# Attention scores by head, the mask carried as extra contraction rows, and row maxima from the high parts only

## The chip, the cores and the metric

The kernel runs on one core of a Trainium2 chip. The metric is the device time of one execution in microseconds (us). Work is spread over five engines that run side by side: TensorE (PE, matmuls; its weight loads are listed as PEld), VectorE (DVE), ScalarE (ACT), GpSimd (POOL) and SyncE (SP), which issues most of the DMA copies.

## The reference

One pre-norm transformer block in float32 over x of shape 4 x 2048 x 256:

```
x = x + attention(layernorm(x), Wq, Wk, Wv, Wo)
x = x + ffn(layernorm(x), W1, b1, W2, b2)
```

Attention has 16 heads of 16 dimensions. A query sees its own position and the 63 before it: `allowed = (j <= i) & (j > i - 64)`; scores are divided by 4 and go through a softmax. The FFN has 1024 hidden units with relu; its weights are rounded to -1, 0 or 1 by `clip(round(W / (mean|W| + 1e-5)))` in the kernel.

## The kernel before

Tokens are cut into 32 chunks of 256 (`C`), eight to a sequence; a chunk has four blocks of 64 queries (`W`, `NB = 4`). Every float32 factor is split into a float16 high part and a float16 low part (`hl`, `ph` and `pl`, `hh` and `hl`, `ht`, `op2`), and a product is the sum of two or three float16 matmuls.

The stages of a chunk, by function:

- `load` and `norm_in`: x comes in as `xt`; `layernorm` (statistics on DVE, a power on POOL at L505, normalisation on DVE at L521 or ACT at L517, high part on ACT at L523, low part on POOL or DVE at L537); a transposing DMA (L545) makes `xT`.
- `project`: q, k and v, twelve matmuls of 256 columns each (L575, L567). High parts are taken on ACT (L619, L585), low parts on DVE (L621, L589). q is written with its block index innermost, so with a step of four float16. q and k go to DRAM (`qd`, `kd`), three copies of 256 rows each, by two DMAs each (L626, L629). v is kept as `vo`, and `ve` is v shifted by one block, made by DMAs (L593, L595, L601).
- `stack`: four DMAs (L650, L656) read q and k back, with the heads in pairs. In `qst` and `kst` a pair has 96 rows: 48 for one head (three high and low combinations of 16 rows) and 48 for the other, with zeros where a head's rows meet the other head's queries. So one matmul gives exact scores of two heads. There are three such buffers (`NQ = 3`), and `stack(c)` waits until the weights of chunk c-3 are done (`used`).
- `maxima`: per block eight matmuls (L675), 128 rows of two heads' queries by 128 keys. The window of 64 keys that a query sees is a ring: a predicated copy (L680) puts the old keys in the place of the new keys that a query may not see, and a reduction (L693) takes the maxima. After four blocks the negated maxima are transposed (L704), copied (L707) and go through DRAM (`md`, issued by ACT at L709 and by POOL at L712) into row 96 of `qst`, where row 96 of `kst` is constant: the next scores come out with their maximum already subtracted.
- `weights`: per block and half of the heads, one matmul writes the mask into the bank (L729, the identity times 512 columns) and four more add transposed scores, keys by queries (L732, 97 rows, 128 columns each):

```
nc.tensor.matmul(tpf, identb, msk.rearrange("p a q -> p (a q)"), start=True, stop=False)
for i in range(4):
    p = g * 4 + i
    nc.tensor.matmul(tp[:, i], ks[0:97, p, b * W:b * W + 128], qs[0:97, p, :, :, b], start=False, stop=i == 3)
```

  ACT takes the exponential and the high part `ph` (L742 and L745, or L751 and L753); the low part `pl` is a subtraction on POOL (L747) or DVE (L755). `lanes.pick` chooses when the program is built.
- `values`: 24 matmuls (L780 to L782) with `ph` and `pl` as stationary operands and v as the moving one; ACT copies out (L787), DVE inverts the sums (L793), POOL multiplies (L805).
- `wo_out`: two transposing DMAs (L828), twelve matmuls (L839), the residual (L843), the second layernorm, a transposing DMA (L855).
- `ffn1` and `ffn2`: the first layer for two chunks at a time (L888 for the bias b1, L892), relu on ACT (L905), low part on DVE (L907); the second layer per chunk (L929, L930) after a one-row product that puts b2 into the bank (L927), the residual (L935) and the store (L938).

The order of the work is not that of the loops. Each stage is a generator that yields what it needs next (an engine with a cost, a buffer, an event); `Lanes.run` plays them against a model of the engines when the program is built, takes the step that can start first, and by `PRIO` among equals. `Lanes.chain` then fixes this order on every engine, SP included. `BUFS` holds the numbers of buffers.

Of the kernel before, what the change touches and what calls it, by code (L numbers as in the profile page):

```python
# [20 lines left out]
D = 256  # L21
# [14 lines left out]
NQ = 3  # L36
NFIRST = 0
NLAST = 6
PRIO = {'norm': -1.1, 'proj': 0.4, 'max': 0.2, 'att': 2.9, 'val': -2.2, 'wo': 0.6, 'ffn': 5.5, 'ffn2': 5.6, 'prep': 3.6}
BUFS = {'xt': 9, 'ln': 2, 'xT': 3, 'zT': 2, 'qk': 4, 'vp': 4, 'pp': 8, 'op': 2, 'av': 2, 'o': 1, 'h': 10, 'r': 7, 'bank': 4, 'lin': 6, 'sp': 2, 'tp': 3, 'pv': 4}  # L40
# [6 lines left out]
WT = {'P': 1.126, 'A': 1.0, 'D': 0.902, 'G': 0.95, 'S': 0.0}  # L47
# [151 lines left out]
def kernel(ctx: ExitStack, tc: tile.TileContext, x, Wq, Wk, Wv, Wo, W1, b1, W2, b2, out):  # L199
# [18 lines left out]
    qkp = pool("qkp", BUFS["qk"])  # L218
# [31 lines left out]
    qd = dram.tile([3, D, NCH * C], HP, name="qd")  # L250
    kd = dram.tile([3, D, NCH * C], HP, name="kd")
    md = dram.tile([NCH, NP, 4 * 2 * W], HP, name="md")
# [3 lines left out]
    identb = const.tile([128, 128], BF, name="identb")  # L256
    mhalf = const.tile([128, NT], FP, name="mhalf")
    zb = const.tile([128, W], FP, name="zb")
    zh = const.tile([48, C], HP, name="zh")
    ones = const.tile([128, 128], FP, name="ones")  # L260
    onesh = const.tile([128, W], HP, name="onesh")


    qst = [const.tile([128, NP, 2, W, 4], HP, name=f"qst{i}") for i in range(NQ)]
    kst = [const.tile([128, NP, W + C], HP, name=f"kst{i}") for i in range(NQ)]
    mst = [const.tile([NP, 128, 4], HP, name=f"mst{i}") for i in range(NQ)]

    b1r = const.tile([33, FF], HP, name="b1r")
    b2r = const.tile([33, D], HP, name="b2r")
# [5 lines left out]
    tri = const.tile([128, W], U8, name="tri")  # L275
    sel = const.tile([128, W], HP, name="sel")
    neg = const.tile([128, W], FP, name="neg")
    mask = const.tile([128, 8, W], BF, name="mask")
    mask0 = const.tile([128, 8, W], BF, name="mask0")

    xts, xTs, vs, ps_, hs, wts = {}, {}, {}, {}, {}, {}
# [3 lines left out]
    def constants():  # L285
        yield "G", 0.4
        make_identity(nc, ident)
        yield "D", 0.6
        nc.vector.memset(mhalf, -0.5)
        nc.vector.memset(zb, 0.0)  # L290
        nc.vector.memset(zh, 0.0)
        nc.vector.memset(ones, 1.0)
        nc.vector.memset(onesh, 1.0)
        signal("const")
        yield "D", 0.3
        nc.vector.tensor_copy(identh, ident)
        nc.vector.tensor_copy(identb, ident)
        signal("ident")

    def masks():  # L300
        yield wait("ident")
        yield "G", 0.8

        for h in range(2):
            r = slice(h * 64, h * 64 + 64)
            nc.gpsimd.affine_select(sel[r], onesh[r], [[1, W]], ALU.is_gt, 0.0, base=0, channel_multiplier=-1)

        mf = const.tile([128, W], FP, name="mf")
        nc.gpsimd.affine_select(mf[0:64], zb[0:64], [[-1, W]], ALU.is_gt, -BIG, base=0, channel_multiplier=1)
        nc.gpsimd.affine_select(mf[64:128], zb[64:128], [[1, W]], ALU.is_ge, -BIG, base=0, channel_multiplier=-1)  # L310
        yield "D", 0.6
        nc.vector.tensor_copy(tri, sel)
        nc.vector.memset(neg, -BIG)
        yield "D", 1.2
        nc.vector.tensor_copy(mask, mf.unsqueeze(1).to_broadcast([128, 8, W]))
        nc.vector.memset(mask0[0:64], -BIG)
        nc.vector.tensor_copy(mask0[64:128], mf[64:128].unsqueeze(1).to_broadcast([64, 8, W]))
        signal("masks")

    def stacks(i):  # L320
        yield wait("const")
        for h in range(2):
            yield "S", (0.65, 1.1)
            nc.sync.dma_start(
                out=qst[i][48 * h:48 * h + 48, :, 1 - h].rearrange("r p q b -> r p (q b)"),
                in_=zh.unsqueeze(1).to_broadcast([48, NP, C]),
            )
        for a in range(0, NP, 2):
            yield "G", 0.57
            nc.gpsimd.memset(kst[i][96:97, a:a + 2], SW * SW)  # L330
        yield "G", 0.5
        nc.gpsimd.memset(mst[i], 0.0)
        signal("used", i - NQ)

# [8 lines left out]
    def weight_qkv(nm):  # L343
# [12 lines left out]
        whv, wlv = wh, wl  # L356
        if nm != "v":
            whv = wh.rearrange("p d (r j) -> p d j r", r=HD)
            wlv = wl.rearrange("p d (r j) -> p d j r", r=HD)
        for d in range(2):  # L360
            wpv = wp[:, d] if nm == "v" else wp[:, d].rearrange("p (j r) -> p j r", r=HD)
            yield "A", 0.3
            nc.scalar.activation(whv[:, d], wpv, AF.Copy, scale=SW)
            yield "D", 0.34
            nc.vector.scalar_tensor_tensor(wlv[:, d], wpv, SW, whv[:, d], ALU.mult, ALU.subtract)
# [4 lines left out]
    def weight_o():  # L370
# [19 lines left out]
        yield "D", 0.6  # L390
# [4 lines left out]
    def biases():  # L395
        yield "G", 0.6
        nc.gpsimd.memset(oner, 1.0)
        nc.gpsimd.memset(b1r, 0.0)
        nc.gpsimd.memset(b2r, 0.0)
        for b, br, n in ((b1, b1r, FF), (b2, b2r, D)):  # L400
# [91 lines left out]
    def layernorm(src):  # L492

        yield wait("const")
        yield "D", 1.07
# [8 lines left out]
        yield "G", 0.63  # L504
# [3 lines left out]
        onact = lanes.pick([[("D", 0.65)], [("D", 0.07), ("A", 1.0)]])  # L508
        xn = rp.tile([128, 2, NT, 128], FP, name="r")
        ht = lnp.tile([128, 2, 2, NT, 128], HP, name="ht")  # L510
        if onact:
            yield "D", 0.07
            nb = small.tile([128, NT], FP, name="nb")
            nc.vector.scalar_tensor_tensor(nb, mv[:, :, 0], -1.0, rs, ALU.mult, ALU.mult)
            for t in range(NT):
                yield "A", 0.5
                nc.scalar.activation(xn[:, :, t, :], src[:, t, :].rearrange("p (d n) -> p d n", d=2), AF.Identity, scale=rs[:, t:t + 1], bias=nb[:, t:t + 1])  # L517
        else:
            yield "D", 0.65
            for t in range(NT):  # L520
                nc.vector.tensor_scalar(xn[:, :, t, :], src[:, t, :].rearrange("p (d n) -> p d n", d=2), mv[:, t, 0:1], rs[:, t:t + 1], ALU.subtract, ALU.mult)  # L521
        yield "A", 0.52
        nc.scalar.copy(ht[:, 0], xn)  # L523
        yield from low([(ht[:, 1], xn, ht[:, 0])], 0.6, 1.11)
# [27 lines left out]
    def project(c, nm):  # L552
# [26 lines left out]
        if nm == "v":  # L579
# [4 lines left out]
            yield "A", 0.48  # L584
# [3 lines left out]
            yield "D", 0.6  # L588
# [21 lines left out]
        yield get("qk")  # L610
        hl = qkp.tile([128, 2, 2, C], HP, name="hl")
        hiv, lov, psv = hl[:, 0], hl[:, 1], ps
        if nm == "q":

            hiv = hl[:, 0].rearrange("p e (q b) -> p e b q", b=4)
            lov = hl[:, 1].rearrange("p e (q b) -> p e b q", b=4)
            psv = ps.rearrange("p e (b q) -> p e b q", b=4)
        yield "A", 0.48
        nc.scalar.copy(hiv, psv)  # L619
        yield "D", 0.6  # L620
        nc.vector.tensor_tensor(lov, psv, hiv, ALU.subtract)  # L621
        put("lin")

        two = 0 if nm == "q" else 1
        yield "S", (0.48, 0.36, 2.05)
        nc.sync.dma_start(out=dst[2 - 2 * two, :, t0:t0 + C].rearrange("(e p) t -> p e t", p=128), in_=hl[:, 0])  # L626
        lanes.cur[0] = lanes.free["S"]
        yield "S", (0.48, 0.73, 2.05)
        nc.sync.dma_start(  # L629
            out=dst[two:two + 2, :, t0:t0 + C].rearrange("s (e p) t -> p (s e) t", p=128),  # L630
            in_=hl.rearrange("p s e t -> p (s e) t"),
        )
        put("qk")
        signal(nm, c)

    def stack(c):
        first = c % NCB == 0
        yield wait("q", c)
        yield wait("k", c)
# [3 lines left out]
        if first:  # L643
            yield "G", 0.46
            nc.gpsimd.memset(ks[0:96, :, 0:W], 0.0)
        lo0 = 0 if first else W
        for ab in range(2):
            rows = slice(48 * ab, 48 * ab + 48)
            yield "S", (0.65, 0.55)
            nc.sync.dma_start(  # L650
                out=qs[rows, :, ab].rearrange("r p q b -> r p (q b)"),
                in_=qd[:, :, t0:t0 + C].rearrange("s (r p a) t -> a (s r) p t", a=2, r=HD)[ab],
            )
            lanes.cur[0] = lanes.free["S"]
            yield "S", (0.65, 0.68)
            nc.sync.dma_start(  # L656
                out=ks[rows, :, W - lo0:],
                in_=kd[:, :, t0 - lo0:t0 + C].rearrange("s (r p a) t -> a (s r) p t", a=2, r=HD)[ab],
            )
            if ab == 0:  # L660
                lanes.cur[0] = lanes.free["S"]
        signal("stack", c)
        for b in range(NB):
            start("max", c, maxima(c, b), 2 * b)
            start("val", c, values(c, b), b)

    def scores(c, b):

        qs, ks = qst[c % NQ], kst[c % NQ]
        yield wait("masks")  # L670
        yield get("sp")
        yield "P", 0.44
        sp = sps.tile([128, NP, 128], FP, name="sp")
        for p in range(NP):
            nc.tensor.matmul(sp[:, p, :], qs[0:96, p, :, :, b], ks[0:96, p, b * W:b * W + 128], start=True, stop=True)  # L675
        yield "D", 0.6
        old = sp[:, :, 0:W]
        if c % NCB == 0 and b == 0:
            old = neg.unsqueeze(1).to_broadcast([128, NP, W])
        nc.vector.copy_predicated(sp[:, :, W:128], tri.unsqueeze(1).to_broadcast([128, NP, W]), old)  # L680
        return sp[:, :, W:128]
# [5 lines left out]
    def maxima(c, b):  # L687
        ring = yield from scores(c, b)
        yield "D", 0.68
        if ("mx", c) not in ps_:  # L690
            ps_["mx", c] = small.tile([128, NB, NP], FP, name="mx")
        mx = ps_["mx", c]
        nc.vector.tensor_reduce(mx[:, b], ring, AX.X, ALU.max)  # L693
        put("sp")
        if not tally(("max", c), NB):
            return
        yield "D", 0.2
        mh = small.tile([128, NB, NP], HP, name="mh")
        nc.vector.tensor_scalar(mh, mx, -1.0 / (SW * SW), PSHIFT * 4.0, ALU.mult, ALU.add)
# [282 lines left out]
```

## Time and profile before

| | |
|---|---|
| median of 3 runs | 903.06 us (901.75 to 903.63) |
| profiled execution, its own time | 909.49 us |
| its span, first to last instruction | 907.8 us |
| mean granted TensorE clock | 0.964 |
| busy share PE / DVE / ACT / POOL | 92 / 66 / 64 / 53% |
| share of the DMA queue of SP (q1) | 57.1% |
| bytes moved by DMA | 110.17 MB |

The profile is of one execution. Busy times of PE overstate its load, since the matmuls are pipelined and their ends overlap: the distance from one start to the next says what a matmul costs. A table by stage gives the busy time of each engine within a window. "Share" of the DMA is the mean over 16 DMA engines, and can exceed 1 in a short window, because an engine has more than one packet in flight.

### The profile page before, as it was taken

How to read it: one execution, taken by the hardware profiler on the slowest of the kernel's cores; microseconds unless marked ns; L12 is line 12 of the kernel's file. 1: busy time of each engine (PE TensorE's matmuls, PEld its weight loads, DVE VectorE, ACT ScalarE, POOL GpSimd, SP SyncE). 2: the span in 40 equal slices, each digit the busy share in tenths (PEclk: the TensorE clock that was granted, in tenths of full speed). 3: DMA queues.
4: the chain of work that ended last, by engine and by line, in shares of the span. 5: the costliest groups of instructions: out<-in, count | busy, mean ns of one | idle time of the engine just before them, and what ended most of it. 6: DMA issues, size and time to landing. Idle time of an engine off the chain costs nothing.

```text
span 907.8 us, 22598 instructions
## 1 busy us (share of the span) xinstructions
PE 834.4 (92%) x8930; PEld 621.2 (68%) x8940; DVE 603.2 (66%) x1231; ACT 583.7 (64%) x1062; POOL 483.6 (53%) x603
## 2 busy tenths in 40 slices
PE   3669989989989999999999999999999899999997
PEld 2557865857748686775858686776858668577774
DVE  7877578386763868758675758658585576746553
ACT  5448975756756676766756776676665666666652
POOL 4418874556535583586446673477536555444220
PEclk9779987989979999999999999999999999999999
DMA  9984882573834737374755737584675467361221
GB/s 227 202 169 102 167 171 46 136 138 71 189 57 117 164 93 171 66 188 73 174 118 117 151 85 156 111 165 85 149 133 112 96 131 158 77 135 25 48 48 35
DMA packets 240846, 110.17 MB, mean 121 GB/s; under 512 B 110081, under 2 KB 238626, under 8 KB 240740
## 3 DMA queue, kind: packets, MB, share of 16 engines
q1 hardware_dynamic: 239204, 108.20, 57.1%
q8 instruction: 70, 1.15, 0.5%
q0 software_dynamic: 1024, 0.26, 0.2%
q10 hardware_dynamic: 512, 0.26, 0.1%
q14 instruction: 36, 0.29, 0.1%
HBM read 39.88 MB, written 33.82 MB: 81 GB/s over the span
## 4 chain that ended last, share of the span: by engine, by line
PE 60%; DMA 10%; DVE 10%; ACT 7%; issue 5%; SPq 4%; POOL 3%; POOLq 0%; ACTq 0%; DVEq 0%
PE bank L732 10%; PE bank L892 10%; PE bank L929 5%; DMA kst<-kd 5%; PE bank L575 5%; PE sp L675 5%; PE bank L930 5%; PE bank L729 5%; PE bank L888 3%; PE bank L839 3%; PE bank L567 2%; PE bank L782 2%; PE bank L780 2%; PE bank L781 2%; ACT hl L619 2%
## 5 line engine op out<-in xcount | busy, mean ns | idle before, releaser
L747 POOL TENSOR_TENSOR pl<-r,ph 128x512 f16<-128x512 f32 x193 | 220.8, 1158 | 94.7 <-ACT ph L745 78.3
L732 PE MATMUL bank<-qst,kst 97*128 97x128 f16 x1024 | 160.2, 291 | 1.8 <-DMA qst<-md 1.2
L892 PE MATMUL bank<-zT,wq 128*128 128x512 f16 (+1 forms) x608 | 142.1, 357 | 0.9 <-DMA zT<-ht 0.9
L905 ACT ACTIVATE hh<-bank 128x512 f16<-128x512 f32 (+1 forms) x152 | 80.1, 530 | 97.4 <-PE bank L892 95.0
L742 ACT ACTIVATE r<-bank 128x512 f32<-128x512 f32 x193 | 113.9, 601 | 43.8 <-PE bank L732 37.3
L732 PEld LDWEIGHTS <-kst 97*128 97x128 f16 x1024 | 111.8, 110 | 44.1 <-issue 12.7
L621 DVE TENSOR_TENSOR hl<-bank,hl 128x512 f16<-128x512 f32 x64 | 62.4, 998 | 83.4 <-ACT hl L619 82.2
L929 PE MATMUL bank<-wq,hh 128*128 128x256 f16 x512 | 117.2, 274 | 0.0
L930 PE MATMUL bank<-wq,hl 128*128 128x256 f16 x512 | 116.5, 273 | 0.0
L745 ACT CAST ph<-r 128x512 f16<-128x512 f32 x193 | 113.5, 624 | 0.4
L805 POOL TENSOR_TENSOR o<-av,rec 64x256 f32<-64x256 f32 x128 | 79.4, 620 | 60.8 <-DVE rec L793 47.5
L907 DVE SCALAR_TENSOR_TENSOR hl<-bank,hh 128x512 f16<-128x512 f32 (+1 forms) x152 | 89.1, 599 | 33.6 <-ACT hh L905 32.8
L680 DVE COPY_PREDICATED sp<-tri,sp 128x512 f32<-128x512 uint8 x124 | 82.8, 694 | 39.8 <-PE sp L675 39.5
L537 POOL TENSOR_TENSOR ht<-r,ht 128x512 f16<-128x512 f32 x58 | 66.9, 1154 | 73.4 <-ACT ht L523 57.6
L729 PE MATMUL bank<-mask,identb 128*128 128x512 bf16 x246 | 97.4, 396 | 6.0 <-ACT av L787 3.0
L505 POOL TENSOR_TENSOR rs<-rs,mhalf 128x2 f32<-128x2 f32 x64 | 45.3, 709 | 105.5 <-DVE rs L503 97.1
L675 PE MATMUL sp<-kst,qst 96*128 96x128 f16 x1024 | 76.5, 227 | 19.0 <-DMA kst<-kd 10.7
L892 PEld LDWEIGHTS <-wq 128*128 128x128 f16 x608 | 47.8, 99 | 65.5 <-issue 35.7
L675 PEld LDWEIGHTS <-qst 96*128 96x128 f16 x1024 | 68.5, 117 | 29.0 <-issue 15.2
L781 PEld LDWEIGHTS <-ph 128*128 128x128 f16 x1024 | 81.1, 97 | 7.6 <-issue 5.5
L780 PEld LDWEIGHTS <-ph 128*128 128x128 f16 x1024 | 83.4, 97 | 1.9
L693 DVE TENSOR_REDUCE mx<-sp 128x8 f32<-128x512 f32 x128 | 83.4, 679 | 0.1
(127 smaller groups left out, 1837.5 us busy)
## 6 DMA issues: line engine op xcount, KB each, us to landing
kst<-kd SPq DMA_DIRECT2D x56, 240.0 KB
qst<-qd SPq DMA_DIRECT2D x64, 192.0 KB
xt<-in_dram SPq DMA_DIRECT2D x36, 256.0 KB
qd<-hl SPq DMA_DIRECT2D x32, 256.0 KB
kd<-hl SPq DMA_DIRECT2D x32, 256.0 KB
out_dram<-xt SPq DMA_DIRECT2D x32, 256.0 KB
ve<-vo SPq DMA_DIRECT2D x32, 136.0 KB
qd<-hl SPq DMA_DIRECT2D x32, 128.0 KB
```

The lines of the kernel that those rows point to most:

```text
L675: nc.tensor.matmul(sp[:, p, :], qs[0:96, p, :, :, b], ks[0:96, p, b * W:b * W + 128], start=True, stop=True)
L729: nc.tensor.matmul(tpf, identb, msk.rearrange("p a q -> p (a q)"), start=True, stop=False)
L732: nc.tensor.matmul(tp[:, i], ks[0:97, p, b * W:b * W + 128], qs[0:97, p, :, :, b], start=False, stop=i == 3)
L742: nc.scalar.activation(pf, tpf, AF.Exp, scale=0.25 / (SW * SW))
L745: nc.scalar.copy(phf, pf)
L747: nc.gpsimd.tensor_tensor(plf, pf, phf, ALU.subtract)
L780: nc.tensor.matmul(pv[:, p, :], ph[:, i, :], v[:, 0, b // 2, p, :], start=True, stop=False)
L781: nc.tensor.matmul(pv[:, p, 0:32], ph[:, i, :], v[:, 1, b // 2, p, 0:32], start=False, stop=False)
L892: nc.tensor.matmul(ps, wq1[:, d, fs], zT[:, i, d, 0:len(grp)], start=False, stop=n == 3)
L907: nc.vector.scalar_tensor_tensor(hl[:, 0:n1], ps, 0.0, hh[:, 0:n1], ALU.max, ALU.subtract)
L929: nc.tensor.matmul(ps[:, t, :], hh[:, ts], wq2[:, f, :], start=False, stop=False)
L930: nc.tensor.matmul(ps[:, t, :], hl[:, ts], wq2[:, f, :], start=False, stop=f == NF - 1)
```

## The change

Scores are now stacked by head, not by pair. A head has 48 rows for the three combinations, one for the maximum (row 48 of a block of 16 that is else zero), and rows 64 to 127 hold the mask: the query side has a one-hot code of the query's place in its block times 60000, the key side 0 or -60000 for that place. The mask product is gone; a weights step is eight matmuls of 128 rows by 64 columns. `kst` holds keys in two windows, for even and odd blocks, since the mask sits at fixed places. The stacks are loaded by nine DMAs of 16 rows, and there are two of them, not three. Rows that never change are set once, in `stacks`.

Row maxima no longer come from the stacks: they use only the high parts of q and k, straight from SBUF. `diagonal` puts q of eight heads on a block diagonal by eight DMAs from SBUF to SBUF; one matmul then gives, for 16 queries of eight heads (128 rows), the scores of 80 keys. Only 16 of the 80 keys need the predicated copy.

Within a block of 64 queries, q is stored with a query's place in its group of 16 outermost. The step that was in writes to SBUF is now in the reads of the accumulators by ACT and DVE: in the q split, and in the exponential or the two instructions after it.

The b2 product is replaced by an addition to the residual on POOL. The weight splits for q and k need no reordering any more. Priorities, numbers of buffers and the planner's costs have new values.

```
-NQ = 3
+NQ = 2
+BIGH = 60000.0
-PRIO = {'norm': -1.1, 'proj': 0.4, 'max': 0.2, 'att': 2.9, 'val': -2.2, 'wo': 0.6, 'ffn': 5.5, 'ffn2': 5.6, 'prep': 3.6}
-BUFS = {'xt': 9, 'ln': 2, 'xT': 3, 'zT': 2, 'qk': 4, 'vp': 4, 'pp': 8, ..., 'r': 7, ...}
+PRIO = {'norm': -2.64, 'proj': -1.41, 'max': 0.28, 'att': 1.3, 'val': 0.75, 'wo': -0.15, 'ffn': 3.66, 'ffn2': 4.57, 'prep': 6.21}
+BUFS = {'xt': 8, 'ln': 2, 'xT': 3, 'zT': 2, 'q': 2, 'k': 3, 'qb': 2, 'vp': 3, 'pp': 6, ..., 'r': 5, ...}
...
     def stacks(i):
+        nc.vector.memset(qbs[i].rearrange("p e b h t -> p (e b h t)"), 0.0)
+        nc.vector.memset(ks[32:64].rearrange("p h w t -> p (h w t)"), SW * SW)
+        nc.vector.memset(qs[32:64].rearrange("p h t -> p (h t)"), 0.0)
+        nc.sync.dma_start(
+            out=ks[64:128].rearrange("p h w (b t) -> p (h w b) t", b=2), in_=kmask[64:128].unsqueeze(1).to_broadcast([64, 4 * H, 128])
+        )
+        nc.scalar.copy(
+            qs[64:128].rearrange("p h (b t) -> p (h b) t", b=NB), qmask[64:128].unsqueeze(1).to_broadcast([64, NB * H, W])
+        )
...
     def project(c, nm):
         if nm == "q":
-            hiv = hl[:, 0].rearrange("p e (q b) -> p e b q", b=4)
-            psv = ps.rearrange("p e (b q) -> p e b q", b=4)
+            hiv, lov = (hl[:, i].rearrange("p e (b q i) -> p (e b) q i", b=NB, i=4) for i in range(2))
+            psv = ps.rearrange("p e (b i q) -> p (e b) q i", b=NB, i=4)
...
+        nc.sync.dma_start(out=dst[:, :, t0:t0 + C].rearrange("s (e p) t -> p (s e) t", p=128), in_=new.rearrange("p s e t -> p (s e) t"))
+            nc.vector.tensor_copy(hl[:, 0, :, 0:W], ks_[c - 1][:, 0, :, C:])
...
+    def diagonal(c, hq):
+        for h in range(8):
+            r = slice(16 * h, 16 * h + 16)
+            nc.sync.dma_start(
+                out=qb[r, :, :, h].rearrange("p e b t -> p (e b) t"), in_=hq[r, 0].rearrange("p e (b t) -> p (e b) t", b=NB)
+            )
...
     def stack(c):
+        for n, s in enumerate((0, 1, 0)):
+            nc.sync.dma_start(out=qs[16 * n:16 * n + 16], in_=qd[s, :, t0:t0 + C].rearrange("(j r) t -> r j t", r=HD))
+        for n, s in enumerate((0, 0, 1)):
+            for w in range(2):
+                a, z = ((t0 - lo0, t0 + C - W) if w == 0 else (t0, t0 + C))
+                nc.sync.dma_start(
+                    out=ks[16 * n:16 * n + 16, :, w, C - (z - a):], in_=kd[s, :, a:z].rearrange("(j r) t -> r j t", r=HD)
+                )
...
     def maxima(c, b):
+        for i in range(4):
+            for e in range(2):
+                nc.tensor.matmul(
+                    sp[:, i, e, 0:80], qb[:, e, b].rearrange("p h t -> p (h t)")[:, i::4],
+                    kw[:, 0, e, b * W + i * 16:b * W + i * 16 + 80], start=True, stop=True,
+                )
-        nc.vector.copy_predicated(sp[:, :, W:128], tri.unsqueeze(1).to_broadcast([128, NP, W]), old)
+        nc.vector.copy_predicated(spf[:, :, 64:80], tri.unsqueeze(1).to_broadcast([128, 8, 16]), spf[:, :, 0:16])
-        nc.vector.tensor_reduce(mx[:, b], ring, AX.X, ALU.max)
+        nc.vector.tensor_reduce(mx[:, :, :, b], sp[:, :, :, 16:80], AX.X, ALU.max)
...
     def weights(c, b, g):
-        nc.tensor.matmul(tpf, identb, msk.rearrange("p a q -> p (a q)"), start=True, stop=False)
-        for i in range(4):
-            nc.tensor.matmul(tp[:, i], ks[0:97, p, b * W:b * W + 128], qs[0:97, p, :, :, b], start=False, stop=i == 3)
+        for i in range(8):
+            nc.tensor.matmul(
+                tp[:, i], ks[:, g * 8 + i, b % 2, b // 2 * 128:b // 2 * 128 + 128], qs[:, g * 8 + i, b * W:b * W + W], start=True, stop=True
+            )
+        tpf = tp.rearrange("p h (q i) -> p h i q", i=4)
...
     def wo_out(c):
+        nc.gpsimd.tensor_tensor(xt, xt, b2b.unsqueeze(1).to_broadcast([128, NT, D]), ALU.add)
...
     def ffn2(grp):
-                        nc.tensor.matmul(ps[:, t, :], oner[:, 0:128], b2r, start=True, stop=False)
```

## Prediction, before the result was known

> **What bounds the kernel now.** I read the page first. TensorE leads, but busy time of pipelined matmuls overstates it, so the page's first part is followed by the table by stage (columns: window; its length; busy us of PE, PEld, DVE, ACT, POOL with counts; clock; DMA share; GB/s):
>
> ```profile
> PE 834.4 (92%) x8930; PEld 621.2 (68%) x8940; DVE 603.2 (66%) x1231; ACT 583.7 (64%) x1062; POOL 483.6 (53%) x603
> ```
>
> ```profile
> 0.00:30.00 30.00, 14.63 (x91) 11.45 (x92) 22.34 (x55) 18.76 (x35) 15.60 (x33) 1.00 0.95 220
> 30.00:60.00 30.00, 18.68 (x145) 14.78 (x143) 24.84 (x51) 8.33 (x13) 6.04 (x11) 0.72 0.89 175
> 450.00:600.00 150.00, 143.70 (x1565) 106.78 (x1567) 102.20 (x215) 98.17 (x174) 82.67 (x101) 1.00 0.62 128
> 830.00:908.00 78.00, 70.91 (x718) 50.07 (x718) 38.14 (x90) 39.31 (x90) 18.54 (x23) 1.00 0.18 39
> ```
>
> The first 60 us belong to the DMA engines (0.95 and 0.89). After that PE is never long idle and everything else is at two thirds. What each PE step costs is read from start to start in the timeline of PE (columns: start, duration, operation, how many):
>
> ```profile
> 429.77 0.28 PE L927 MATMUL bank<-b2r,oner 33*128 33x256 f16 x1
> 429.98 0.28 PE L929 MATMUL bank<-wq,hh 128*128 128x256 f16 x1
> 430.10 0.27 PE L930 MATMUL bank<-wq,hl 128*128 128x256 f16 x1
> ...
> 500.53 0.40 PE L729 MATMUL bank<-mask,identb 128*128 128x512 bf16 x1
> 500.76 0.62 PE L732 MATMUL bank<-qst,kst 97*128 97x128 f16 x4
> 501.21 0.40 PE L729 MATMUL bank<-mask,identb 128*128 128x512 bf16 x1
> ...
> 503.22 1.06 PE L675 MATMUL sp<-kst,qst 96*128 96x128 f16 x16
> 504.11 0.38 PE L567 MATMUL bank<-wvh,xT 128*128 128x256 f16 x2
> ...
> 505.48 0.18 PE L782 MATMUL bank<-ve,pl 128*128 128x34 f16 x1
> 505.50 0.18 PE L780 MATMUL bank<-ve,ph 128*128 128x34 f16 x1
> 505.53 0.18 PE L781 MATMUL bank<-ve,ph 128*128 128x32 f16 x1
> ```
>
> A weights step takes 501.21 - 500.53 = 0.68 us: 0.23 for the mask product, then 0.45 for four products of 128 columns, 113 ns each. Sixteen maxima products of the same 128 columns take 0.89 us, 56 ns each. The two differ in the moving operand: L732 streams qst with the block index innermost, every fourth element; L675 streams kst contiguously (its strided operand is the stationary one). So a strided stream costs double. The value products, each with its own 128x128 weight load, go every 25 ns. The b2 product costs 0.21 us.
>
> Per chunk of 256 tokens, from such starts: projections 3 x 12 x 109 ns = 3.9 us, maxima 4 x 0.445 = 1.8, weights 8 x 0.68 = 5.4, values 4 x 0.61 = 2.4, output projection 1.3, first FFN layer 5.2 (1.29 per step for two chunks), second 2 x (0.21 + 16 x 0.109) = 3.9, transposes 0.3: 24.2 us. The span is about 60 us of start, 15 of end, and 32 periods of 26.0 us: PE issues for 93% of a period. It is the bound.
>
> **What the change removes from PE.**
> - The mask product (256 of them) goes; eight products of 64 contiguous columns replace four strided ones of 128. From 109 ns for 256 columns and 216 for 512 (L892's starts) comes 0.42 ns a column and about 2 ns: 29 ns each, 0.235 us a step in place of 0.68, 3.6 us per chunk. [...] The value rows show load and product together in 25 ns, with 34 columns and the same 128x128 stationary: the row decides, 29 ns.
> - Maxima: eight products again, of 80 columns, not 128. Stream alone 36 ns; the stationary operand is strided as before, and L675 bounds that at 56. I take 45: 0.35 us per chunk (0 to 0.64).
> - The b2 products: 2 x 0.21 = 0.4 us per chunk.
>
> PE falls to 24.2 - 4.35 = 19.9 us per chunk.
>
> **The other engines, per chunk.**
> - DVE has 603/32 = 18.8. The predicated copy shrinks from 512 to 128 elements a row. The rows of L907 (680 ns for 512, 422 for 256) give about 1 ns an element and 164 ns fixed, so 692 becomes about 295 ns: -1.6. The q split wrote every fourth f16: the pair of q and k has a median of 998 ns over 632 to 1356, so q costs about 1.31 and k 0.69. Now it writes contiguously: -0.6. The copy of 64 old keys adds 0.15. Result 16.8. All resets of the stacks are extra at the start: 16,384 f16 per row and buffer, some 7 us each by the 165 ns of a 128x128 f32 memset.
> - ACT has 18.2: -0.7 for q (969 ns median over 564 to 1362, the same pair), -0.7 for mst, which wrote strided at 1.29 us. 16.8. It also issues a second md transfer (0.27 us).
> - POOL has 15.1 and gets the b2 addition, priced by the other 128x512 f32 subtraction, 1.16 us: 16.3. It is hidden: xt is next needed by L935, after the whole FFN of that chunk. If POOL were full, the planner's choice puts `pl` on DVE (0.69 us).
> - SP: a chunk issues 13 copies and 4 transposes, now 24 copies: one write each for q and k (two before), eight copies for the diagonal, nine stack loads (four before). By the SP rows (0.4 to 0.65 a copy, 1.26 a transpose) 12.2 us becomes 18.2. SP is in order: behind a waiting stack load stand the next chunk's xT and oT transposes, then PE.
> - The gpsimd load of the maxima row must wait for the weights of chunk c-2, no longer c-3, with POOL's `pl` subtractions queued behind it. Before it waited 3.2 us for PE in all and 38.9 for md. I take +0.5 us per chunk on POOL (0 to 2).
> - New priorities and buffer counts reorder everything; no row prices that. At most it wins the idle 7% of PE, and could lose as much: ±1.8 us per chunk, taken at nothing.
>
> **The DMA queue** is where I expect the gain to be eaten. Its share in the steady stages is about 0.59 of 26: 15.3 us per chunk. One stack, with its four loads:
>
> ```profile
> 512.00:517.40 5.40, 5.40 (x35) 2.04 (x35) 5.33 (x18) 2.46 (x6) 2.46 (x5) 1.00 0.96 180
> 517.40:519.00 1.60, 1.60 (x22) 0.70 (x17) 1.06 (x4) 0.82 (x2) 1.31 (x2) 1.00 0.00 0
> ```
>
> ```profile
> kst<-kd SPq DMA_DIRECT2D x56, 240.0 KB
> qst<-qd SPq DMA_DIRECT2D x64, 192.0 KB
> ```
>
> 2 x 192 + 2 x 240 = 864 KB in about 5.3 us, 163 GB/s, engines full, into 48 partitions a load. The new loads write 16 partitions each, three for q and six for k (both windows): 1,180 KB. At the row's 163 GB/s that is 7.2 us. [...] No load of 16 partitions is in this trace. [...] The diagonal copies move 131 KB in pieces of 128 bytes, 0.7 us at 180 GB/s, taken double: +1.4. The dropped third copies of q and k save 256 KB, -1.1. DMA comes to 20.3 us per chunk, level with PE.
>
> **Sum.** Before, one resource ran at 93% of a period. Now DMA (20.3), PE (19.9) and SP (18.2) are tied, over one another's waits; I take 88%: 23.0 us. The start, bound by DMA, gets two mask broadcasts of 1 MB for six zero fills of 192 KB, the resets and the longer first stack: +9. So 69 + 32 x 23.0 + 15 = 820 us of span. The profiled execution took 909.49 us (span 907.8), 0.7% above the median of 903.06. Carried over to the median: 815.
>
> **Rivals.**
> - *PE stays alone at the top.* If the 16-partition loads overlap, DMA is 17.5 and hidden, and PE keeps 93%: 21.4 us a period, 685 + 84, about 765. For it: the DMA share of 0.6 leaves room today. Against: the start shows DMA full as soon as loads bunch. 0.18.
> - *Strided PSUM reads make ACT the bound, and the kernel slower.* The new exp, or the cast after it, and the q cast read PSUM at a stride of 16 or 64 bytes, nine per chunk. No row reads PSUM so. Lower bound: nothing (PE's strided stream still ran at 0.88 ns an element, about ACT's own pace). Upper: strided writes. q's 8-byte stride cost +0.71 us, and L363's 32-byte stride 1267 against 384 ns for 256 elements, +1.76 for 512. [...] At +0.71 ACT is 23.2 and the time about 880; it decides from +0.82 us a read (ACT at 24.2), and at +1.76 gives 1,190. 0.15, of which 0.10 slower.
> - *DMA or SP saturates.* [...] 0.12, of which 0.05 slower, 0.02 equal.
>
> The likeliest case has 0.55. Faster by over 0.2% (about what a measurement of this kernel tells from no change): 0.55 + 0.18 + 0.05 + 0.05 = 0.83; within it 0.02; slower 0.15. The range of 755 to 900 leaves out some 0.05 below and the slower cases above.
>
> **What would show it.** Right: a weights step of 0.24 us from start to start; PE busy below 85% with the DMA share above 0.8; stack loads landing later; predicated copies near 295 ns; exp at 600 ns. Wrong: exp or cast above 1.3 us (second rival), weights products at 56 ns or more (weight loads bind), PE still at 95% in the middle (first rival), a clock well under 0.96 from a PE that starves.

## The result and the profile after

The change makes the kernel slower: 972.11 us (970.59 to 977.18) against 902.82, a ratio of 1.078 (95% interval 1.074 to 1.082). Forecast were 815 us, in a range of 755 to 900. Times below are medians of all executions, and the ratios leave out executions in the chip's slower state, of which there is one, of 847.91 us among the four of the version at 840 below (median without it 835). The profiled execution has a span of 975.3 us. Its page, with the queue's line of before beneath (packets, MB, share of 16 engines), and its table by stage, in the columns of before:

```profile
PE 748.4 (77%) x9644; PEld 547.2 (56%) x9644; DVE 571.9 (59%) x1271; ACT 534.8 (55%) x1055; POOL 529.8 (54%) x633
...
q1 hardware_dynamic: 291720, 114.48, 81.5%
```

```profile
q1 hardware_dynamic: 239204, 108.20, 57.1%
```

```profile
0.00:30.00 30.00, 9.81 (x50) 7.39 (x51) 22.29 (x27) 16.43 (x30) 6.97 (x16) 0.97 0.74 196
...
450.00:600.00 150.00, 127.90 (x1577) 87.87 (x1576) 92.39 (x203) 87.13 (x170) 87.53 (x103) 0.85 0.83 121
600.00:750.00 150.00, 119.16 (x1565) 86.69 (x1562) 89.62 (x208) 84.80 (x167) 83.40 (x100) 0.87 0.91 127
```

No compute engine is full any more, and PE falls from 143.7 to 127.9 busy us in the stage from 450 to 600, in part at a halved clock (0.85 granted on average there). What is nearly full is the DMA: its engines are occupied for 0.83 to 0.91 of the time, at 121 to 127 GB/s, no more than the 128 GB/s of before at a share of 0.62. More occupied for the same flow: the packets have become slower. On the mean one occupies an engine for 43.6 ns (81.5% of 16 engines' 975.3 us, over 291,720 packets), against 34.7 before (57.1% of 907.8 us, over 239,204). There are also 22% more of them, with 6% more bytes.

PE's part of the change did what it was meant to do. The timeline of PE, and the views of one line's instructions (durations min/median/max, then first and last start), L766 and L732 being the weights products after and before:

```profile
607.95 0.86 PE L766 MATMUL bank<-qst,kst 128*128 128x64 f16 x24
```

```profile
L766 PE MATMUL bank<-qst,kst x2048: 189/193/261, 92.1 to 935.0; 128*128 128x64 f16 x187
```

```profile
L732 PE MATMUL bank<-qst,kst x1024: 274/294/314, 65.5 to 868.7; 97*128 97x128 f16 x171
```

```profile
L779 ACT ACTIVATE r<-bank x189: 570/598/658, 92.7 to 912.0; 128x512 f32<-128x512 f32 x189
```

```profile
L720 DVE COPY_PREDICATED sp<-tri,sp x128: 265/286/297, 76.4 to 908.7; 128x128 f32<-128x128 uint8 x128
```

Twenty-four products in 0.86 us, of which the last takes 0.19: (0.86 - 0.19)/23 = 29 ns each, so a step of eight in 0.23 us. The exponential with the strided read of the accumulator takes 598 ns, as before without it (597). The predicated copy takes 286 ns. But the first weights product starts at 92.1 us, not at 65.5, and the periods after it are longer. Counted by the starts of L766 in order (64 to a chunk), the weights of chunk 8 begin at 294 us and those of chunk 28 at 858: 28.2 us a period, against 26.05 before (265 to 786, 32 products of L732 to a chunk).

What PE waited for longest (line and what released it; us in total, times, longest):

```profile
PE bank L933 <- DMA zT<-ht: 39.0, 12, 6.9
PE sp L710 <- DMA qb<-hq: 32.3, 9, 7.8
PE bank L876 <- DMA oT<-op: 30.6, 20, 7.6
PE bank L575 <- DMA xT<-ht: 22.6, 7, 9.8
```

These are the transposing copies for the FFN, the output projection and the next projections, and the copies of the diagonal (`qb`): 124.5 us in all, where the kernel before shows 0.9. The stack loads themselves hardly appear among PE's waits. They cost by holding up what is issued behind them: with their rows spread, below, the 124.5 us fall to 79.3.

The wait shown here costs PE twice, for after it the clock is at 0.50. The timeline (in brackets the idle time before, and what ended it) and the stage around it:

```profile
615.57 0.60 PE L929 MATMUL bank<-oner,b1r 33*128 33x512 f16 x1 [6.75 <-DVE vo L589]
617.79 1.49 PE L766 MATMUL bank<-qst,kst 128*128 128x64 f16 x24
```

```profile
611.70:621.90 10.20, 6.33 (x37) 3.05 (x38) 6.49 (x18) 2.83 (x6) 3.60 (x4) 0.50 0.99 189
```

The 24 products that took 0.86 us at 607.95 take 1.49 here, at a granted clock of 0.50. Over the whole execution the mean clock is 0.859, against 0.964 before. The clock records of the two traces have the values 1.00 and 0.50 alone; 275 us of the span are at 0.50 here, against 65 before (2 x 0.141 x 975.3 and 2 x 0.036 x 907.8 give the same).

One period of the change, in the timeline of SP (start, duration, line, how many) and in the table by stage for three stretches of it:

```profile
505.81 3.25 SPq L651 DMA_DIRECT2D qb<-hq  x4
509.10 0.65 SPq L595 DMA_DIRECT2D ve<-vo  x1
509.79 1.89 SPq L651 DMA_DIRECT2D qb<-hq  x3
511.73 0.64 SPq L601 DMA_DIRECT2D ve<-vo  x1
512.46 1.27 SPq L545 DMA_TRANSPOSE xT<-ht  x1
515.69 1.35 SPq L677 DMA_DIRECT2D qst<-qd  x3
517.08 5.09 SPq L687 DMA_DIRECT2D kst<-kd  x6
522.42 1.87 SPq L892 DMA_TRANSPOSE zT<-ht  x1
524.40 0.51 SPq L627 DMA_DIRECT2D qd<-hq  x1
525.01 2.44 SPq L627 DMA_DIRECT2D kd<-hk  x1
```

```profile
507.50:510.00 2.50, 2.50 (x7) 0.54 (x5) 2.50 (x3) 1.37 (x4) 2.50 (x3) 0.50 0.25 48
511.00:513.00 2.00, 2.00 (x8) 0.87 (x8) 1.54 (x5) 0.77 (x3) 2.00 (x2) 0.58 0.17 25
517.50:526.50 9.00, 9.00 (x115) 6.20 (x113) 7.00 (x16) 6.33 (x13) 6.58 (x11) 1.00 1.23 107
```

There are two opposite states. While SP issues the eight copies of the diagonal (L651; the first had gone out at 498.71), at 0.6 to 0.8 us each for 16 KB, the DMA engines are nearly idle in the two stretches shown (0.25 and 0.17). PE isn't idle there: at a clock near half its 2.50 busy us are just seven long products. While the nine stack loads run, the engines are over-full (1.23) and yet bring 107 GB/s; the stack of before came at 180. SP then waits too: a write takes it 2.44 us to issue.

### The profile page after: what moved, and what is told of

Its sections match the earlier page's. It is cut to its first block, busy times and chain, and to the rows that moved or that the text cites. A ratio compares the mean times of both kernels' runs of the same rounds, so it can differ in the third digit from the quotient of the medians.

```text
span 975.3 us, 24492 instructions
## 1 busy us (share of the span) xinstructions
PE 748.4 (77%) x9644; PEld 547.2 (56%) x9644; DVE 571.9 (59%) x1271; ACT 534.8 (55%) x1055; POOL 529.8 (54%) x633
## 3 DMA queue, kind: packets, MB, share of 16 engines
q1 hardware_dynamic: 291720, 114.48, 81.5%
q8 instruction: 75, 1.23, 0.6%
## 4 chain that ended last, share of the span: by engine, by line
PE 32%; DMA 25%; POOL 12%; DVE 10%; SPq 8%; issue 8%; ACT 4%; POOLq 0%; ACTq 0%; DVEq 0%
PE bank L933 8%; DMA zT<-ht 5%; POOL pl L784 5%; PE bank L575 4%; DMA xt<-in_dram 4%; PE bank L876 4%; DMA qb<-hq 3%; PE bank L968 3%; DMA qst<-qd 2%; PE bank L766 2%; PE bank L969 2%; DMA oT<-op 2%; SPq L651 2%; PE bank L929 2%; DMA kst<-kd 2%
## 5 line engine op out<-in xcount | busy, mean ns | idle before, releaser
L933 PE MATMUL bank<-zT,wq 128*128 128x512 f16 (+1 forms) x608 | 163.5, 398 | 39.0 <-DMA zT<-ht 39.0
L779 ACT ACTIVATE r<-bank 128x512 f32<-128x512 f32 x189 | 106.1, 602 | 64.3 <-PE bank L766 45.2
L766 PE MATMUL bank<-qst,kst 128*128 128x64 f16 x2048 | 95.0, 201 | 22.1 <-DMA qst<-md 8.0
L842 POOL TENSOR_TENSOR o<-av,rec 64x256 f32<-64x256 f32 x128 | 79.3, 620 | 42.8 <-DVE rec L830 31.3
L766 PEld LDWEIGHTS <-kst 128*128 128x128 f16 x2048 | 83.8, 103 | 29.8 <-issue 18.0
L537 POOL TENSOR_TENSOR ht<-r,ht 128x512 f16<-128x512 f32 x64 | 74.1, 1158 | 48.3 <-ACT ht L523 40.0
L710 PE MATMUL sp<-hk,qb 128*128 128x80 f16 x1024 | 60.1, 215 | 43.9 <-DMA qb<-hq 32.3
L824 ACT COPY av<-bank 128x272 f32<-128x272 f32 x128 | 49.5, 388 | 68.6 <-PE bank L819 67.3
L819 PEld LDWEIGHTS <-pl 128*128 128x128 f16 x1024 | 81.1, 97 | 7.4 <-POOL pl L784 5.6
L575 PE MATMUL bank<-xT,wqh 128*128 128x256 f16 x256 | 53.9, 313 | 38.3 <-DMA xT<-ht 22.6
L521 DVE TENSOR_SCALAR r<-xt,mv,rs 128x256 f32<-128x256 f32 x112 | 81.3, 766 | 3.3 <-POOL rs L505 2.3
```

What stands on the lines that cost most here:

```text
L575: nc.tensor.matmul(ps[:, e, :], a[:, d, es], xT[:, i, d], start=n == 0, stop=n == 5)
L766: nc.tensor.matmul(tp[:, i], ks[:, g * 8 + i, b % 2, b // 2 * 128:b // 2 * 128 + 128], qs[:, g * 8 + i, b * W:b * W + W], start=True, stop ...
L779: nc.scalar.activation(pf.rearrange("p (h i q) -> p h i q", h=8, i=4), tpf, AF.Exp, scale=0.25 / (SW * SW))
L933: nc.tensor.matmul(ps, wq1[:, d, fs], zT[:, i, d, 0:len(grp)], start=False, stop=n == 3)
```

## The experiments

Three theories. Q: loads into 16 neighbouring partitions are slow and hold the DMA queue. S: SP's in-order issuing binds, the copies of the diagonal above all. D: two stacks instead of three, fewer buffers and another order. Ratios below are to the kernel before, run on the same chip, with their 95% intervals.

**Which partitions a load writes.** First every third row, then rows dealt out by fours:

```
-out=qs[16 * n:16 * n + 16]      -out=ks[16 * n:16 * n + 16, :, w, C - (z - a):]
+out=qs[n:48:3]                  +out=ks[n:48:3, :, w, C - (z - a):]        (every third)
+out=qs[n:64:4]                  +out=ks[n:64:4, :, w, C - (z - a):]        (by fours)
```

Every third: 

> The changed kernel, but the nine stack loads of a chunk write every third of 48 partitions each (rows n, n+3, ...) and not 16 neighbouring ones; number, bytes and pieces of the loads are the same. Theory Q (loads into 16 neighbouring partitions are slow, 512-byte pieces at about 100 ns, and hold the one DMA queue for 11 us per chunk): pieces fall to 50-70 ns, a stack to 6-7 us, and the time from 972 to 850-890 us. Rival S (SP issues 28 transfers a chunk in order, and the eight copies of the diagonal hold it for 5 us with the DMA engines idle): within 1% of 972. Rival D (two stacks instead of three, fewer buffers, the new order): within 1% of 972.

Measured: 941.86 us, ratio 1.042 (1.037 to 1.047): 30 us gained, a third of what Q expected. In the stage from 450 to 600 us the DMA engines stayed as occupied as in the change (0.84 against 0.83), at 129 GB/s in place of 121. Why these rows gain no more is not shown, and the run alone does not decide Q.

By fours: 

> The changed kernel with the stack's rows dealt out by fours: a load writes partitions n, n+4, ... n+60, so that its 16 rows are spread evenly over 64 partitions; number, bytes and pieces of the loads, and all products, stay (the constant rows are set over 64 rows, the zero fill of a sequence's first chunk falls away, the maximum goes to row 51). Theory Q (what is slow is that 16 neighbouring partitions, or an uneven spread as with every third row, crowd on few ways into the memory): pieces of 512 bytes near 30-40 ns, the DMA share at 0.6, the time as with half the bytes, 850-875 us. Rival B (the bytes themselves, or the count of pieces, are too many): like every third row, 935-972 us.

Measured: 878.39 us, ratio 0.973 (0.967 to 0.980): 94 us less than the change, just above the expected range, with the same number of transfers, bytes and pieces, and with the order of the work kept. Its SP timeline, the table by stage over that stack's loads and over the same long stage, and the queue's line:

```profile
504.12 1.89 SPq L676 DMA_DIRECT2D qst<-qd  x3
506.06 0.64 SPq L601 DMA_DIRECT2D ve<-vo  x1
506.74 5.00 SPq L686 DMA_DIRECT2D kst<-kd  x6
```

```profile
504.50:511.50 7.00, 7.00 (x65) 4.31 (x64) 5.84 (x14) 4.00 (x8) 4.60 (x6) 1.00 0.71 166
```

```profile
450.00:600.00 150.00, 129.06 (x1824) 96.71 (x1824) 103.65 (x233) 98.30 (x194) 100.46 (x118) 0.95 0.68 144
```

```profile
q1 hardware_dynamic: 291720, 114.48, 60.4%
```

The same 114.48 MB in the same 291,720 packets take 60.4% of a shorter span, not 81.5%, and a stack comes at 166 GB/s, now at the pace at which SP issues. A packet is down to 28.9 ns of an engine's time on the mean, by the same sum as above. Rival B of the expectation (bytes or pieces) falls as the main cost. What the run shows is the effect of the rows; why one choice of rows is slower than another is in no view here, and the ways into the memory stay the author's guess.

**Half the bytes.** From the third chunk on, each load moves 8 of 16 heads: `nh = H if c < NQ else H // 2`.

> The changed kernel, but from the third chunk on each of the nine stack loads moves 8 of the 16 heads (half the bytes, the same number of transfers); the other heads keep old rows, and the exponential's scale is 0 so that nothing overflows. Theory Q: a stack falls from 11 to about 5.5 us and the time to 850-890 us, as with the spread rows. Rival S: the number of issues is the same, 955-972 us. Rival D: within 1% of 972.

Measured: 853.81 us, ratio 0.945 (0.940 to 0.950), with q1 at 55.8%. It agrees with Q, and lies 25 us below the run by fours, so fewer bytes gain something too, on the queue or in SP's issuing.

**Narrow loads in the kernel before.** Each of its four stack loads becomes three of 16 neighbouring partitions.

> The kernel before with one suspect put in: each of its four stack loads of 48 partitions is cut into three of 16 neighbouring partitions, the same 864 KB, eight more issues on SP. Theory Q: 640-byte pieces rise to 100 ns and more, a stack takes 8-9 us in place of 5.3, the DMA share goes from 0.59 to 0.75, and the kernel gets 1-5% slower, 910-950 us, since its queue still has room. Rival D (depth of two and the new order, not the loads): within 1% of 903.

Measured: 915.92 us, ratio 1.015 (1.009 to 1.022). The time is as expected, but not the reason: the share of the queue fell instead of rising.

```profile
q1 hardware_dynamic: 243300, 108.22, 51.7%
```

Its loads move 64 to 80 KB each. If SP issues one in 0.65 us, the mean for the stack loads of the kernel before (676 ns for q, 618 for k), that is an estimated 100 to 125 GB/s: the queue keeps up at a share of 51.7%, and what this run pays may be its eight further issues per chunk. The changed kernel sends 128 KB per load, faster than that (three in 1.35 us at 515.69). So it seems that not a narrow load as such fills the queue, but a burst of them beyond about 107 GB/s. This reading is worked out from the two runs and not shown; no run varied the pace alone.

**Spread rows in the kernel before**, over every second of 96 partitions: 

> The kernel before with the 48 rows of each head of a pair dealt out over every second of 96 partitions; the same loads, bytes and pieces. Theory Q: 640-byte pieces fall from 53 to about 40 ns, a stack from 5.3 to about 3.5 us, the DMA share from 0.59 to 0.53; PE bounds this kernel, so the time falls little: 885-903 us. Rival B: nothing changes.

Measured: 895.07 us, ratio 0.990 (0.987 to 0.993). Small, as expected where PE is the bound.

**Who issues the diagonal's copies.** `nc.sync.dma_start` becomes `nc.scalar.dma_start` in `diagonal`. The first try also told the planner:

> The changed kernel, but the eight copies of the block diagonal are issued by ACT (0.25 us each, +2 us of ACT per chunk), not by SP. Theory Q: the 11 us of stack loads stay, so at most 2% faster, 950-975 us. Rival S: SP gets 5 us of each chunk's 28 back, 850-880 us. Rival D: within 1% of 972.

Measured: 1006.03 us, ratio 1.114 (1.107 to 1.122), slower than the change itself. Taken alone, this would have refuted S. But the planner, given other costs, had made another order of everything (POOL's busy time fell from 530 to 432 us). So the edit was repeated with the planner's entry for SP left in place, on the kernel with rows by fours and then on the change as it is:

> The changed kernel with rows dealt out by fours (878 us), and the eight copies of the block diagonal issued by ACT, with the planner's order kept. Rival S in its second place (with the loads spread, SP's 21 us of issuing in a period of 25 bind): SP falls to 16 us, 840-862 us. If not, or if ACT's products wait behind the copies: 875-900 us.

Measured: 840.06 us, ratio 0.928 (0.920 to 0.937): 38 us less than with SP.

> The changed kernel with its loads as they are (16 neighbouring partitions), and the eight copies of the block diagonal issued by ACT with the planner's order kept. With the loads spread the same edit gave 38 us (878 to 840). If the slow loads and SP's issuing add up as separate costs: 972 falls to 930-945 us. If the slow loads hide SP's part (the queue is then the bound, and SP waits on it anyhow): 960-975 us.

Measured: 929.04 us, ratio 1.030 (1.025 to 1.036): 43 us less than the change.

```profile
450.00:600.00 150.00, 124.49 (x1727) 93.89 (x1726) 93.49 (x219) 90.67 (x178) 92.38 (x112) 0.92 0.98 136
```

In this last kernel the queue in the same stage is at 0.98: the idle stretches are filled, the over-full ones stay. The two costs add up, in the time and in PE's waits for the four kinds of copy named above (in brackets, us):

| | copies issued by SP | by ACT |
|---|---|---|
| loads of 16 neighbouring partitions | 972 (124.5) | 929 (76.0) |
| rows dealt out by fours | 878 (79.3) | 840 (38.8) |

The mean clock rises along with it: 0.859, 0.901 with ACT, 0.921 by fours, 0.933 with both. So some of each gain may be the clock; no run held it fixed. The edit also moves the copies to another queue (q10 carries 4.47 MB in place of 0.26), where they no longer stand behind SP's loads. Whether the 43 us are SP's issuing time or that place in the queue, no run separates.

The copies are as dear to issue on ACT (median 593 ns), not 0.25 us as I had assumed from the md transfers:

```profile
L651 ACTq DMA_DIRECT2D qb<-hq x256: 592/593/2290, 20.5 to 739.4; - x128
```

Half on each engine, `(nc.scalar if h % 2 else nc.sync).dma_start`: 

> The changed kernel with rows dealt out by fours, and four of the eight diagonal copies issued by ACT and four by SP, order kept. The run with all eight on ACT took 840 us; there one such issue held ACT for 0.6-0.7 us, 173 us in all, not the 0.25 that was assumed, so ACT was occupied for 727 of 831 us and SP for 511. If ACT's issuing costs there: 820-836 us. If SP is the tighter one still: 845-862 us.

Measured: 836.60 us, ratio 0.926 (0.923 to 0.929). This is at the edge of the forecast and cannot be told from 840, so neither engine's issuing seems to bind by then. It is the fastest version here, 7.4% faster than the kernel before.

**Two stacks in the kernel before**, `NQ = 2` and nothing else: 

> The kernel before with two stacks instead of three and nothing else (NQ = 2; the planner makes its order for that). Rival D (the depth): stack loads can start only when the weights of chunk c-2 are done, and the time rises by 3-8%, 930-975 us. Theory Q: PE's products of another chunk fill the gap; within 2% of 903.

Measured: 944.07 us, ratio 1.046 (1.041 to 1.051). Depth, with the order that the planner makes for it, costs here. What SP waited for before it could issue a stack load (L650), first in the kernel before, then with two stacks:

```profile
SPq L650 <- PE bank L732: 10.5, 5, 6.7
```

```profile
SPq L650 <- PE bank L732: 52.0, 17, 6.8
```

PE's own wait for the key loads, before the maxima, goes from 10.7 to 44.1 us.

With spread rows as well: 

> The kernel before with two stacks (944 us), and its rows dealt out over every second of 96 partitions (which alone, with three stacks, gave 1%). If the depth costs because a stack's load now lies between the weights of chunk c-2 and those of chunk c, a load that takes 2 us less gives 20-40 us here: 905-925 us. If depth and load time have nothing to do with one another: 1% here as well, 932-942 us.

Measured: 929.65 us, ratio 1.027 (1.023 to 1.031). 1.5% is gained by spreading, against 1% with three stacks. Depth and the time of a load hang together only weakly, if at all. In both kernels with `NQ = 2` the planner also made another order, so 4.6% is depth with its order. What three stacks would do for the changed kernel was not tried.

**The start.** The constant rows of the key stacks are set by POOL, two f16 at a time (3.5 us each in place of 6.9 us on DVE). First with the planner told so, on the change and on the version by fours:

> The changed kernel, but the rows of constants in the two key stacks are set by POOL, as pairs written as one 32-bit word (half the count), not by DVE, where each took 6.9 us between 15 and 31 us with the first layernorms and q splits queued behind. Theory Q+R (besides the loads, these resets hold up the start): the first weights product moves from 92 to about 72-80 us and the time from 972 to 950-962 us, the later periods unchanged. Rival (the start is bound by DMA or by SP, whose issue of a 256 KB load took 9 us there): the first weights product stays within 4 us of 92 and the time within 0.7% of 972.

Measured: 999.45 us, ratio 1.106 (1.101 to 1.112). The first weights product came 13 us earlier, at 79 us, and the kernel got 27 us slower.

> The changed kernel with both remedies: stack rows dealt out by fours (the run that gave 878 us) and the constants of the key stacks set by POOL. If the start is worth 12-20 us there too: 858-868 us; if it is hidden: 874-880.

Measured: 891.00 us, ratio 0.985 (0.979 to 0.992), slower than 878.

> The same with both remedies, and the eight copies of the block diagonal issued by ACT. Rival S in its second place: with the loads spread, SP is busy issuing for 21 us of each period of 25, 5 of them for these copies. If SP is now the bound: 3-6% faster than the kernel with both remedies, 815-845 us. If these copies are late behind the stack loads whoever issues them, or block ACT: no faster or slower, 860-900 us.

Measured: 876.29 us, ratio 0.972 (0.966 to 0.978): 1.6% faster than the run before it.

With the order kept: 

> The changed kernel; POOL, not DVE, sets the constant rows of the key stacks (half the count), and the planner keeps its old entry for DVE, so that the order of all else is the one of the changed kernel. In the run before, the planner was told, and made another order: its first weights product came at 79 us instead of 92, and yet it took 999 us. If that loss was the new order: the start is won and kept, 955-966 us. If what the start gains is lost in later periods anyhow, because the queue is the bound: 968-975 us.

Measured: 975.01 us, ratio 1.078 (1.073 to 1.083).

> The same edit, with the planner's order kept, on the changed kernel with rows dealt out by fours (878 us). If the start counts there: 862-871 us. If not: 875-881.

Measured: 884.18 us, ratio 0.977 (0.973 to 0.981). In both the first weights product starts where it did (93 and 85 us, against 92 and 83), so in this order the resets are not what makes the start late, and the expectation that they were is refuted. SP's timeline shows it held for 8.4 us by the two mask broadcasts (L330) and then for 9.1 us by one load of x (L488) behind them; no run took these away.

**The kernel before with contiguous q.** The stack becomes [pair, block, head, query], so that the weights products stream without a stride:

```
-qst = [const.tile([128, NP, 2, W, 4], HP, name=f"qst{i}") for i in range(NQ)]
+qst = [const.tile([128, NP, 4, 2, W], HP, name=f"qst{i}") for i in range(NQ)]
-    qs[0:97, p, :, :, b]
+    qs[0:97, p, b]
```

> The kernel before, with one edit: q keeps its block index outside in the stacks ([pair, block, head, query]), so the weights products stream contiguously, and the q split and the copy of the maxima write contiguously. The stack's q loads then have pieces of 128 bytes, four times as many. From the profile of before: L732 falls from 113 to 56 ns (58 us of PE in all), ACT loses 45 us, DVE 20 us. If PE bounds the kernel before, 845-870 us; if the small pieces of the q load (3,072 a chunk) are dear on the queue, 880-910.

Measured: 893.97 us, ratio 0.988 (0.982 to 0.994). PE's busy time falls from 834 to 783 us, the kernel's by 9 only. The q loads have become 128-byte pieces, and q1 rises to 65.8%. That the queue takes the rest of PE's gain is an inference, which the next run supports in part. With spread rows:

> The kernel before with contiguous q in the stacks (as in the run that gave 894 us) and the rows dealt out over every second of 96 partitions. Theory Q: the queue's share falls from 0.69 to about 0.6 and the 58 us that PE lost come out: 850-875 us. Rival B: 890-897 us as without the spread.

Measured: 879.51 us, ratio 0.975 (0.969 to 0.981), 14 us less, but short of the 850 to 875 of the expectation.

## Why the prediction was wrong

The step that failed is the one from the engines' sums to a period: DMA (20.3 us), PE (19.9) and SP (18.2) were taken to run side by side, with the largest filling 88% of 23.0 us. The period is 28.2 us. In it slow loads and SP's small copies take turns, and PE waits and runs at half clock for a part. By term:

- *PE.* Right at full clock. A step takes 0.23 us as forecast, weight loads do not bind (29 ns for a product of 64 columns with its own load), and the maxima run at 36 ns (16 in 0.74 us), at the lower end of 36 to 56. The second rival (strided reads on ACT) is refuted: the sum had these reads at nothing, which no run of before shows, and the exponential took 598 ns against 597.
- *The clock.* Put at nothing. A clock well under 0.96 stood among the signs of being wrong, but in no term of the sum. It came: 0.859, or 275 us at half clock. How much of the loss that is by itself stays open.
- *DVE, ACT, POOL.* The durations are right: 286 ns for 295 forecast, 0.57 us for the copy of the maxima. The b2 addition takes 1.28 us, not 1.16.
- *DMA, 20.3 us per chunk.* Mis-sized, and this is the largest error that a run shows. Its mean share of 0.87 over the stages from 300 to 750 us makes 0.87 x 28.2 = 24.5 us, four more. Of the 20.3 us 10 stand for the stack, 4.7 more than before, and no run of before shows that term: its trace has no load of 16 partitions. In the change the stack shown kept the engines over-full for about 9 us (1.23 from 517.5 to 526.5), at 107 GB/s. What the sum left out is that for this time what stands behind the stack comes late, the transposes that PE needs above all. Spreading the rows shows what this is worth: 94 us, of which 9 lie before the first weights product; the period falls from 28.2 to 24.8 us.
- *SP, 18.2 us per chunk.* Mis-sized: 702 us of issuing in all, 21.9 per chunk. A copy of the diagonal takes 0.67 us on the mean, not 0.4 to 0.65, and issues behind a full queue stretch: a write of k took 2.44 us at 525.01, one at 43.48 took 0.51. Moving these copies to ACT gains 43 us.
- *The tie at 88%.* This step failed in its form. DMA, SP and PE were treated as running beside one another, so that the largest sets the period. SP's small copies and the slow loads instead take turns on one in-order path: the DMA engines idle at 0.2 during the first, SP waits during the second. The table of four times shows that they add. My third rival (DMA or SP saturates, a chance of 0.12) had the right place; 28.2 us a period was measured.
- *The depth.* I named the wait for chunk c-2 for the row of maxima only, at 0.5 us on POOL, and took the new order and buffers at nothing. In the kernel before two stacks with their order cost 42 us. That much of it is in the changed kernel is not shown: its maxima no longer read the stacks, and what is left is SP's wait for the weights products before a stack load, 32.2 us in all.
- *The start, +9 us.* The first weights product is 27 us late. The resets, which I had named, are not the cause with the order kept. Nor does DMA bind the first 30 us as it did: its share there is 0.74, against 0.95 before. The cause of these 27 us stays open, and they are more than a third of the 69 us by which the kernel got slower.
- *The signs.* PE below 85%, a DMA share above 0.8, a step of 0.24 us, copies near 295 ns and exponentials at 600 were to show that I was right, and all came true. They fit the third rival as well, so they could not tell it from the likeliest case.

Without the two costs that the runs remove, the change gives 837 to 840 us, 3% above the 815 that was forecast. That is partly luck: at 840 the DMA share of 300 to 750 us is 0.70 of a period of 23.3 us, which makes 16.4 us per chunk and not 20.3, so the period of 23.0 is nearly met by another sum.

## What to carry to other kernels

When bytes move between engines and buffers, cost the transfers by the partitions that they write and by what their issue holds up, not by bytes: here 94 us lay in which 16 rows a load wrote, at equal bytes. The small copies and the slow loads on one in-order queue added up here (38 to 43 us for the copies, 89 to 94 for the rows); they did not overlap merely because different columns of the table show them. And where a planner makes the order, an experiment must keep that order: the same edit to who issues eight copies read +3.5% with a new order and -4.4% with the old one.

## What was not expected of the hardware

- An issue of a copy of 16 KB into 16 partitions holds its engine for about 0.6 us, on SP (599 ns median) as on ACT (593 ns); the 4 KB md transfers take ACT 0.25 us.
- The DMA share rose to 1.23 in a stretch that moved 107 GB/s, and stood at 0.71 in one that moved 166: the share shows how long packets occupy the engines, not flow. Only the two columns together tell a full queue from a slow one.
- ACT's read of the accumulator at a 16-byte stride cost nothing (598 ns against 597), while its write of every fourth f16 had cost 1.31 us, for q in the kernel before, against 0.59 for k.
